# Layer norms cut into 128-token steps, and the last pair of sequences finished in halves

## The chip, the core and the metric

The kernel runs on one core of a Trainium2 chip. A core has five engines with their own instruction queues: PE (matrix products), DVE (vector), ACT (scalar functions), POOL (GpSimd) and SP (here only the issuer of transfers). Each queue runs strictly in order; engines wait for one another through semaphores. Products land in PSUM, which has eight banks of 128 x 512 float32 values; everything else lies in SBUF. The metric is the device time of one execution in microseconds.

## What is computed

Sixteen sequences of 256 tokens with 128 features go through twelve layers of attention without softmax, each with a residual sum, then a layer norm, a gated feed-forward part and a second layer norm:

```python
for i in range(12):
    q, k, v = split(x @ Wqkv[i].T + bqkv[i])          # 16 heads of 8
    att = einsum('bhqd,bhkd->bhqk', q, k) / sqrt(8)
    y = einsum('bhqk,bhkd->bhqd', att, v)
    x = y @ Wproj[i].T + bproj[i] + x
x = layernorm(inputs + x)
h = silu(x @ wg.T) * (x @ wu.T)                        # 384 hidden, weights int / 127
x = layernorm(x + h @ wd.T)
```

Because there is no softmax, the kernel carries, for each sequence, a 128 x 128 matrix that maps the input tokens to the current ones (and one column for the offset), and multiplies the tokens by it only at the end.

## The kernel before

Sequences are taken in eight pairs (p = 0 to 7, 512 tokens each). A prologue computes for each pair the Gram matrix of its tokens (L328), with a column of ones beside the tokens so that the same product gives the token sums. DVE turns them into means (L332 to L334), PE turns the means into rows (L338), and DVE makes the centred Gram matrix g (L345). Twelve layers follow, in two groups of four pairs. Then `ffn` runs once for each pair.

In `ffn`, 512 tokens are four chunks of 128 (K = 4). PE applies the pair's matrix to the tokens (L627 and L629) into one bank; `norm(pr, True)` is the first layer norm. It has three operations: statistics of the four chunks, either all on ACT (L568, squares with an accumulated sum) or all on DVE (four L571 and then four L573); the reciprocal root on POOL (L580 and L581); and the scaling, either on DVE in one instruction over 512 columns (L586) or on ACT in four (L591). PE transposes the result (L635); a copy (L637, ACT or DVE) and a difference on DVE (L638) split it in a high and a low part so that reduced-precision float32 products stay exact. For each of three blocks of 128 hidden units PE makes gate and up (L645, L646), ACT the silu (L648), DVE the product with up (L649), ACT or DVE the high part (L650), POOL or DVE the low part (L651), and PE adds both parts' products to the down bank (L656 to L658). DVE adds the residual (L660), PE transposes back (L664), and `norm(po, False)` is the second layer norm: statistics on DVE alone (L571, L573), the root on POOL, an offset on DVE (L599), and the scaling of the four chunks, all on DVE (L593) or all on ACT (L595). One transfer writes the pair's 512 tokens (L668).

The order of the instructions is not written out. Every operation is handed to `Plan` with a modelled cost for each engine that may run it, the values that it reads and writes, and a priority. `Plan.run` (L113) always takes, among the operations that could end first, the one with the lowest priority number less a small share of the work that hangs on it, gives it to the engine on which it would end first, and emits it there. The priority of a pair's `ffn` is L + FOFF + FSTEP * p (L692), with FSTEP = 0.15. The plan knows of the eight banks only who may hold one: it has no rule on which engines may read one bank at the same time. The semaphores are put in afterwards, by the layer under the kernel, from the tiles that each instruction touches. What stands outside the plan (constants, masks, the memsets of the ones at L265) is placed by that layer.

Of the kernel before, what the change touches and what calls it, by code (L numbers as in the profile page):

```python
# [9 lines left out]
F32 = mybir.dt.float32  # L10
# [3 lines left out]
AF = mybir.ActivationFunctionType  # L14
ALU = mybir.AluOpType
# [6 lines left out]
C = 128  # L22
# [21 lines left out]
LATE = 0.02  # L44
QLATE = 0.3
FOFF = -1
FSTEP = 0.15
LSTEP = 0.05
WLEAD = 0.6
TAILW = 0.0001  # L50
# [38 lines left out]
class Plan:  # L89
    def __init__(self, slots):  # L90
        self.slots, self.ops = slots, []

    def op(self, costs, emit, reads=(), writes=(), prio=0.0):

        o = Op(len(self.ops), costs, emit, prio)
        for v in reads:
            o.deps.update(v.writers)
        for v in writes:
            o.deps.update(v.writers, v.readers)
            v.writers, v.readers = [o], []  # L100
        for v in reads:
            if v not in writes:
                v.readers.append(o)
        o.vals = list(dict.fromkeys([*reads, *writes]))
        for v in o.vals:
            if v.kind:
                v.left += 1
                v.ops.append(o)
        for d in o.deps:
            d.users.append(o)  # L110
        self.ops.append(o)
# [49 lines left out]
def mm32(n=C):  # L161
    return max(220, 4 * n / 2.4 + 8)


def mmr(n):
    return max(111, 0.447 * n + 5)


def act(n, sbuf=False, pointers=0):
    return (94 if sbuf else 51) + 93 * pointers + n / 1.2  # L170


def dve(n, fast=False):
    return 69 + n / (1.92 if fast else 0.96)


def pool(n):
    return 147 + 2.1 * n
# [7 lines left out]
def linear_attention_ffn_kernel(ctx: ExitStack, tc: tile.TileContext, x, xt, wall, wq0, bias, wg, wu, wd, out):  # L186
# [9 lines left out]
    def copy(e, dst, src):  # L196
        if e == ACT:
            nc.scalar.copy(dst, src)  # L198
        else:
            (nc.vector if e == DVE else nc.gpsimd).tensor_copy(dst, src)  # L200

    def sub(e, dst, a, b):
        (nc.vector if e == DVE else nc.gpsimd).tensor_tensor(dst, a, b, ALU.subtract)  # L203
# [5 lines left out]

    zero = new("zero", [128], BF16)  # L210
    nc.vector.memset(zero, 0.0)
    for _ in range(WARM):
        nc.tensor.matmul(banks[7][:, :128], zero, zero, start=True, stop=True)
    tst = new("tst", [B, W])
# [43 lines left out]
        plan.op({SP: kb * 5}, lambda e: nc.sync.dma_start(dst, src), [], vs, prio)  # L258


    qgvs = [new(f"qgv{p}", [PB * W + PB * C]) for p in range(NP)]
    xtoks = [t.rearrange("p (k c) -> p k c", c=C + 1) for t in qgvs]
    vq, vgv = [Val() for _ in range(NP)], [Val() for _ in range(NP)]
    for p in range(NP):
        nc.gpsimd.memset(xtoks[p][:, :, C:], 1.0)  # L265
        load(xtoks[p][:, :, 0:C], x[p * 512 : (p + 1) * 512, :].rearrange("(k p) c -> p k c", p=128), [vq[p], vgv[p]], -9 + 0.01 * p)
        load(xts[p], xt[:, p * PB * T : (p + 1) * PB * T], [vx[p]], 2 + 0.01 * p)

# [279 lines left out]
    def ffn(p, prio):  # L548
# [5 lines left out]
        v = {n: Val() for n in ("cr", "cp", "cq", "tt", "st", "rs", "nb", "x1", "xh", "xl", "sg0", "sg1", "hh0", "hh1", "hl0", "hl1")}  # L554
        v["cp"], v["cq"] = vcp[p % 2], vcq[p % 2]

        def op(costs, emit, reads, writes):
            plan.op(costs, emit, reads, writes, prio)

        def norm(src, centred):  # L560

            xs, rows = t("x1"), lambda: bank(src)
            cut = lambda a, k: a[:, k * C : (k + 1) * C]

            def stats(e):
                if e == ACT:
                    for k in range(K):
                        nc.scalar.activation(cut(xs, k), cut(rows(), k), AF.Square, scale=1 / math.sqrt(C), accum_out=t("mv")[:, k, 1:2])  # L568
                else:
                    for k in range(K):  # L570
                        nc.vector.bn_stats(t("st")[:, k, :], cut(rows(), k))  # L571
                    for k in range(K):
                        nc.vector.bn_aggr(t("mv")[:, k, :], t("st")[:, k, :])  # L573
            costs = {DVE: K * (dve(C) + 70)}
            if centred:
                costs[ACT] = K * (act(C) + 93)
            op(costs, stats, [src], [v["st"], v["x1"]])

            def rstd(e):
                nc.gpsimd.tensor_scalar(t("ve"), t("mv")[:, :, 1], 1.0, EPS, ALU.mult, ALU.add)  # L580
                nc.gpsimd.tensor_tensor(t("rs"), t("ve"), mhalf, ALU.pow)  # L581
            op({POOL: 1220}, rstd, [v["st"]], [v["rs"]])

            def scale(e):
                if centred and e == DVE:
                    nc.vector.tensor_tensor(chunks(xs), chunks(rows()), t("rs").unsqueeze(2).to_broadcast([128, K, C]), ALU.mult)  # L586
                    return
                for k in range(K):
                    d, r, rs = cut(xs, k), cut(rows(), k), t("rs")[:, k : k + 1]
                    if centred:  # L590
                        nc.scalar.activation(d, r, AF.Copy, scale=rs)  # L591
                    elif e == DVE:
                        nc.vector.tensor_scalar(d, r, t("mv")[:, k, 0:1], rs, ALU.subtract, ALU.mult)  # L593
                    else:
                        nc.scalar.activation(d, r, AF.Identity, bias=t("nb")[:, k : k + 1], scale=rs)  # L595
            if centred:
                costs = {DVE: dve(N), ACT: K * act(C, False, 1)}
            else:
                op({DVE: 75}, lambda e: nc.vector.scalar_tensor_tensor(t("nb"), t("mv")[:, :, 0], -1.0, t("rs"), ALU.mult, ALU.mult), [v["rs"], v["st"]], [v["nb"]])  # L599
                costs = {DVE: K * 319, ACT: K * act(C, False, 2)}  # L600
            op(costs, scale, [src, v["rs"], v["st"], v["nb"]], [v["x1"]])


        ptt, pc, pr, px, pd, po = (Val("bank") for _ in range(6))

        def tr_t(e):
            for b in range(PB):
# [20 lines left out]
            for k in range(K):  # L628
                nc.tensor.matmul(bank(pr)[:, k * C : (k + 1) * C], x[:, k * 128 : (k + 1) * 128], t("tt")[:, (k // 2) * C : (k // 2 + 1) * C], start=False, stop=(k == K - 1))  # L629
        op({PE: K * mm32() + mmr(N)}, mm_r, [vx[p], v["tt"], v["cq"]], [pr])  # L630
        norm(pr, True)

        def tr_x(e):
            for k in range(K):
                nc.tensor.transpose(bank(px)[:, k * 128 : (k + 1) * 128], t("x1")[:, k * C : (k + 1) * C], ident)  # L635
        op({PE: K * 109}, tr_x, [v["x1"]], [px])
        op({ACT: act(N), DVE: dve(N)}, lambda e: copy(e, t("xh"), bank(px)), [px], [v["xh"]])  # L637
        op({DVE: dve(N)}, lambda e: nc.vector.tensor_tensor(t("xl"), bank(px), t("xh").bitcast(F32), ALU.subtract), [px, v["xh"]], [v["xl"]])  # L638
        for n in range(NH):
            sg, hh, hlo = f"sg{n % 2}", f"hh{n % NB}", f"hl{n % NB}"  # L640
            pgate, pup = Val("bank"), Val("bank")
            for key, o in (("g", pgate), ("u", pup)):
                def mm_x(e, key=key, o=o, n=n):
                    ws = fw[key][:, n * C : (n + 1) * C]
                    nc.tensor.matmul(bank(o), ws, t("xh"), start=True, stop=False)  # L645
                    nc.tensor.matmul(bank(o), ws, t("xl"), start=False, stop=True)  # L646
                op({PE: 2 * mmr(N)}, mm_x, [v["xh"], v["xl"], vfw[key]], [o])
            op({ACT: act(N)}, lambda e, sg=sg, o=pgate: nc.scalar.activation(t(sg), bank(o), AF.Silu, scale=QSCALE), [pgate], [v[sg]])  # L648
            op({DVE: dve(N)}, lambda e, sg=sg, o=pup: nc.vector.scalar_tensor_tensor(t(sg), bank(o), QSCALE, t(sg), ALU.mult, ALU.mult), [pup], [v[sg]])  # L649
            op({ACT: act(N, True), DVE: dve(N, True)}, lambda e, sg=sg, hh=hh: copy(e, t(hh), t(sg)), [v[sg]], [v[hh]])  # L650
            op({POOL: pool(N), DVE: dve(N)}, lambda e, sg=sg, hh=hh, hlo=hlo: sub(e, t(hlo), t(sg), t(hh).bitcast(F32)), [v[sg], v[hh]], [v[hlo]])  # L651

            def mm_d(e, n=n, hh=hh, hlo=hlo):
                ws = fw["d"][:, n * C : (n + 1) * C]
                if n == 0:
                    nc.tensor.matmul(bank(pd), id127r, t("xl"), start=True, stop=False)  # L656
                nc.tensor.matmul(bank(pd), ws, t(hh), start=False, stop=False)
                nc.tensor.matmul(bank(pd), ws, t(hlo), start=False, stop=(n == NH - 1))  # L658
            op({PE: (2 + (n == 0)) * mmr(N)}, mm_d, [v[hh], v[hlo], v["xl"], vfw["d"]], [pd])
        op({DVE: dve(N)}, lambda e: nc.vector.scalar_tensor_tensor(t("sg0"), bank(pd), QSCALE, t("xh").bitcast(F32), ALU.mult, ALU.add), [pd, v["xh"]], [v["sg0"]])  # L660

        def tr_o(e):
            for k in range(K):
                nc.tensor.transpose(bank(po)[:, k * C : (k + 1) * C], t("sg0")[:, k * 128 : (k + 1) * 128], ident)  # L664
        op({PE: K * 109}, tr_o, [v["sg0"]], [po])
        norm(po, False)
        r0 = p * N
        op({SP: 2.6 * N}, lambda e: nc.sync.dma_start(out[r0 : r0 + N, :].rearrange("(k p) c -> p k c", p=128), chunks(t("x1"))), [v["x1"]], [])  # L668

    prep_weights(0)  # L670
    for p in range(NP):
# [54 lines left out]
```

## Time and profile before

| | |
|---|---|
| median of three runs | 320.36 us (319.89 to 320.46) |
| profiled execution | 319.71 us |
| its span | 317.5 us |
| busy: PE, DVE, ACT, POOL | 304.1, 242.2, 216.2, 142.4 us |
| mean granted PE clock | 0.989 |
| writes of the output | 8 transfers of 256 KB, median 2.3 us from issue to landing |

The span runs from the first to the last recorded event; some 2.2 us of the execution lie outside it. The stages are: the prologue to about 20 us, the layers to about 259 us (the last addition into the sequences' matrices, L516, starts at 259.25 us), the feed-forward parts, which overlap the last layer and go on to about 307 us on PE, and the rest of the norms and the last write. In an answer by line a line of code may stand for a helper: L198, L200, L203 and L206 are copies, differences and products of the kind that the tile names say.

### The profile page before, as it was taken

The page shows a single profiled execution, that of the slowest core. Times are in us where ns is not written, and L with a number is a line of the kernel's source. Part 1 is how long each engine was busy: PE and PEld are TensorE (multiplying, and loading weights), DVE is VectorE, ACT ScalarE, POOL GpSimd, SP SyncE. Part 2 cuts the span into 40 slices and gives each one's busy share as a digit, 9 for nine tenths or more (in the row PEclk, how much of TensorE's full clock was granted, in tenths as well). Part 3 has the DMA queues.
Part 4 walks back from the last instruction along what each step waited for, and adds up shares of the span by engine and source line. Part 5 has one row for each costly group of instructions (what it writes and reads, how often), then busy time and mean ns, then how long its engine had stood idle before and what let it go on. Part 6 is the DMA issues. An engine that isn't in the chain of part 4 may idle for free.

```text
span 317.5 us, 12581 instructions
## 1 busy us (share of the span) xinstructions
PE 304.1 (96%) x5074; PEld 279.8 (88%) x5074; DVE 242.2 (76%) x743; ACT 216.2 (68%) x579; POOL 142.4 (45%) x239
## 2 busy tenths in 40 slices
PE   6999999999999999999999999999999999999970
PEld 6998999999999999999999999999999898888840
DVE  4779688767777677776877768677597698999995
ACT  2458887676776767667676676767687677957651
POOL 6327543326433364233641436313431356658863
PEclk9999999999999999999999999999999999999995
DMA  7463640210201103021030110310000000001124
GB/s 224 111 197 96 173 118 2 51 39 16 72 2 39 51 8 81 2 51 39 2 87 2 39 51 2 76 52 5 3 2 2 2 4 0 2 0 33 35 79 121
DMA packets 22473, 15.64 MB, mean 49 GB/s; under 512 B 1936, under 2 KB 19856, under 8 KB 22416
## 3 DMA queue, kind: packets, MB, share of 16 engines
q1 hardware_dynamic: 22128, 14.75, 17.1%
q8 instruction: 40, 0.66, 0.9%
q14 instruction: 17, 0.14, 0.2%
q10 hardware_dynamic: 288, 0.09, 0.1%
HBM read 8.02 MB, written 2.10 MB: 32 GB/s over the span
## 4 chain that ended last, share of the span: by engine, by line
PE 93%; DVE 4%; POOL 2%; issue 0%; DVEq 0%; POOLq 0%
PE bank L443 14%; PE bank L422 8%; PE bank L492 8%; PE bank L424 7%; PE bank L423 7%; PE bank L482 5%; PE bank L430 5%; PE bank L509 4%; PE bank L510 4%; PE bank L511 4%; PE bank L645 3%; PE bank L432 3%; PE bank L646 3%; PE bank L431 3%; PE bank L328 3%; PE bank L375 3%
## 5 line engine op out<-in xcount | busy, mean ns | idle before, releaser
L203 POOL TENSOR_TENSOR thl<-tst,thl 128x260 fp32r<-128x260 f32 x88 | 68.5, 809 | 32.4 <-ACT thl L198 32.4
L198 ACT COPY qgv<-bank 128x256 f32<-128x256 f32 x174 | 63.0, 373 | 25.6 <-PE bank L432 18.2
L198 ACT COPY kv<-bank 128x512 f32<-128x512 f32 (+1 forms) x92 | 52.4, 573 | 21.1 <-PE bank L424 8.2
L422 PE MATMUL bank<-whl,thl 128*128 128x256 f32 x176 | 51.9, 295 | 0.0
L423 PE MATMUL bank<-whl,thl 128*128 128x256 f32 x176 | 49.5, 281 | 0.0
L424 PE MATMUL bank<-whl,thl 128*128 128x256 f32 x176 | 49.4, 281 | 0.0
L390 POOL TENSOR_SCALAR tst<-tst,bcol 128x8 f32<-128x8 f32 x21 | 7.0, 332 | 94.0 <-PE bank L375 94.0
L443 PE MATMUL bank<-kv,g 128*128 128x128 f32 x352 | 42.9, 275 | 0.0
L198 ACT CAST thl<-tst 128x260 fp32r<-128x260 f32 x88 | 32.3, 409 | 15.3 <-DVE tst L516 15.1
L443 PEld LDWEIGHTS bank<-kv,g 128*128 128x128 f32 x352 | 41.1, 191 | 0.2 <-issue 0.2
L516 DVE TENSOR_TENSOR tst<-bank,tst 128x260 f32<-128x260 f32 x96 | 36.2, 424 | 5.2 <-POOL tst L390 3.2
L200 DVE CAST yhl<-bank 128x260 fp32r<-128x260 f32 x48 | 18.3, 423 | 27.3 <-PE bank L492 27.3
L436 DVE TENSOR_SCALAR qgv<-bank,bcol 128x2 f32<-128x2 f32 x88 | 19.3, 220 | 25.5 <-ACT qgv L198 20.8
L422 PEld LDWEIGHTS bank<-whl,thl 128*128 128x128 f32 x176 | 33.1, 188 | 4.2 <-issue 4.2
L505 DVE TENSOR_TENSOR yhl<-bank,yhl 128x260 fp32r<-128x260 f32 x96 | 34.2, 418 | 0.0
L423 PEld LDWEIGHTS bank<-whl,thl 128*128 128x128 f32 x176 | 33.2, 189 | 0.0
L424 PEld LDWEIGHTS bank<-whl,thl 128*128 128x128 f32 x176 | 33.2, 188 | 0.0
L430 PE MATMUL bank<-thl,whl 128*128 128x260 f32 x88 | 29.0, 330 | 0.0
L492 PE MATMUL bank<-qgv,gm 32*32 32x130 f32 x1536 | 25.9, 280 | 0.0
L198 ACT CAST yhl<-bank 128x260 fp32r<-128x260 f32 (+1 forms) x56 | 20.6, 411 | 7.6 <-PE bank L492 5.9
L432 PE MATMUL bank<-thl,whl 128*128 128x260 f32 x88 | 24.7, 281 | 0.0
L431 PE MATMUL bank<-thl,whl 128*128 128x260 f32 x88 | 24.7, 281 | 0.0
(155 smaller groups left out, 739.0 us busy)
## 6 DMA issues: line engine op xcount, KB each, us to landing
wraw<-wall SPq DMA_DIRECT2D x12, 256.0 KB, 3.4
wpt<-whl SPq DMA_DIRECT2D x24, 96.0 KB, 2.2
qgv<-x SPq DMA_DIRECT2D x8, 256.0 KB, 5.4
xt<-xt SPq DMA_DIRECT2D x8, 256.0 KB, 4.7
out<-kv SPq DMA_DIRECT2D x8, 256.0 KB, 2.3
wpt<-whl SPq DMA_DIRECT2D x24, 64.0 KB, 2.2
wpt<-whl SPq DMA_DIRECT2D x24, 32.0 KB, 1.9
wraw<-wg SPq DMA_DIRECT2D x1, 192.0 KB, 3.8
```

Source lines behind the costliest of these rows:

```text
L198: nc.scalar.copy(dst, src)
L203: (nc.vector if e == DVE else nc.gpsimd).tensor_tensor(dst, a, b, ALU.subtract)
L422: nc.tensor.matmul(o, hi[:, b, 0:C], hl(0, 1, 2), start=True, stop=False)
L423: nc.tensor.matmul(o, hi[:, b, 0:C], hl(1, 1, 2), start=False, stop=False)
L424: nc.tensor.matmul(o, lo[:, b, 0:C], hl(0, 1, 2), start=False, stop=True)
L430: nc.tensor.matmul(o, hl(0, 0), flat(hi), start=True, stop=False)
L431: nc.tensor.matmul(o, hl(0, 0), flat(lo), start=False, stop=False)
L432: nc.tensor.matmul(o, hl(1, 0), flat(hi), start=False, stop=True)
L443: nc.tensor.matmul(bank(pgv)[:, b * C : (b + 1) * C], g0[p][:, b, :], tv(b), start=True, stop=True)
L492: nc.tensor.matmul(bank(pys[r])[group(g + r), b * W : (b + 1) * W], gm[group(g), r * PB + b, :], qss[p][group(g), b, :], start=True, stop= ...
L505: plan.op({DVE: dve(PB * W)}, lambda e: nc.vector.tensor_tensor(yl, bank(py)[:, : PB * W], yh.bitcast(F32), ALU.subtract), [py, vyh[p]], [ ...
L516: plan.op({DVE: dve(PB * W)}, lambda e: nc.vector.tensor_tensor(ts, bank(pw)[:, : PB * W], ts, ALU.add), [pw], [vt[p], vc[p]], prio)
```

## The change

Four things change.

First, `norm` hands the plan each chunk's statistics and each chunk's scaling as an operation of its own. So the chunks of one norm may go to different engines. On DVE a chunk's aggregate (L573) now follows its own statistics (L571) at once, where four of the one were followed by four of the other; the DVE scaling of the first norm is one instruction a chunk in place of one for all four.

Second, the last pair (p = 7) has its third hidden block, its down product, its residual sum, its transposes, its second norm and its output in two halves of 256 tokens. Each half has a down bank and a transpose bank of its own. In this third block the down product is a plain float32 product of the whole value, with no high and low part.

Third, FSTEP goes from 0.15 to 0.3, and the last pair's second and third block and its end get a priority number lower by FLAST = 0.2, which the plan takes sooner.

Fourth, the ones beside the tokens are set by DVE, in the code right after the first memset, and no longer by POOL.

```diff
-FSTEP = 0.15
+FSTEP = 0.3
+FLAST = 0.2
...
     nc.vector.memset(zero, 0.0)
+    qgvs = [new(f"qgv{p}", [PB * W + PB * C]) for p in range(NP)]
+    xtoks = [t.rearrange("p (k c) -> p k c", c=C + 1) for t in qgvs]
+    for t in xtoks:
+        nc.vector.memset(t[:, :, C:], 1.0)
...
-        nc.gpsimd.memset(xtoks[p][:, :, C:], 1.0)
...
-        def norm(src, centred):
+        def norm(src, centred, ks, x1):
...
+            for k, vk in zip(ks, vs):
+                def stats(e, k=k):
+                    if e == ACT:
                         nc.scalar.activation(cut(xs, k), cut(rows(), k), AF.Square, scale=1 / math.sqrt(C), accum_out=t("mv")[:, k, 1:2])
+                    else:
                         nc.vector.bn_stats(t("st")[:, k, :], cut(rows(), k))
                         nc.vector.bn_aggr(t("mv")[:, k, :], t("st")[:, k, :])
-            costs = {DVE: K * (dve(C) + 70)}
+                costs = {DVE: dve(C) + 90}
...
+            for k, vk in zip(ks, vn):
+                def scale(e, k=k):
                     d, r, rs = cut(xs, k), cut(rows(), k), t("rs")[:, k : k + 1]
+                    if e == DVE and centred:
+                        nc.vector.tensor_scalar(d, r, rs, None, ALU.mult)
...
+                costs = {DVE: dve(C) + 60, ACT: act(C, False, 1)} if centred else {DVE: 319, ACT: act(C, False, 2)}
+                op(costs, scale, [src, rs, *vs, nb], [vk])
...
+        halves = [range(K // 2), range(K // 2, K)] if p == NP - 1 else whole
+        pds = [pd] if len(halves) == 1 else [Val("bank") for _ in halves]
         for n in range(NH):
+            parts = halves if n == NH - 1 else whole
+            if p == NP - 1 and n:
+                sooner[0] = FLAST
+            for i, ks in enumerate(parts):
...
+                if plain:
+                    def mm_f(e, n=n, sg=sg, ks=ks, j=i):
+                        nc.tensor.matmul(cols(bank(pds[j]), ks), fw["d"][:, n * C : (n + 1) * C].bitcast(F32), cols(t(sg), ks), start=False, stop=True)
+                    op({PE: mm32(m)}, mm_f, [s, vfw["d"], v[sg]], [pds[i]])
+                    continue
...
+        for i, ks in enumerate(halves):
+            y, po = Val(), Val("bank")
...
+            x2 = norm(po, False, ks, [v["xl"]])
+            r0, r1 = (p * K + ks[0]) * 128, (p * K + ks[-1] + 1) * 128
+            op({SP: 2.6 * m}, lambda e, ks=ks, r0=r0, r1=r1: nc.sync.dma_start(out[r0:r1, :].rearrange("(k p) c -> p k c", p=128), chunks(cols(t("x1"), ks))), x2, [])
```

## The prediction

> **What bounds the kernel.** I read the shares and slices of the page first. PE is busy 96% of the span, so up to about 305 us the kernel seems bound by PE. I then asked for the engines' busy time from the last addition into the sequences' matrices (L516, 259.25 us) on. The columns are start and end, length, then PE, PEld, DVE, ACT and POOL busy.
>
> ```profile
> 259.25:270.00 10.75, 10.75 (x81) 9.24 (x79) 9.90 (x29) 8.68 (x37) 7.62 (x23) 1.00 0.00 2
> 270.00:306.90 36.90, 35.95 (x174) 28.82 (x172) 36.15 (x103) 26.90 (x58) 27.83 (x27) 1.00 0.08 22
> 306.90:314.20 7.30, 1.32 (x9) 0.84 (x8) 7.01 (x34) 1.50 (x4) 3.00 (x5) 0.73 0.45 124
> 314.20:317.50 3.30, 0.00 (x0) 0.00 (x0) 0.00 (x0) 0.00 (x0) 0.00 (x0) 0.50 0.43 123
> ```
>
> From there DVE is busy 9.90 + 36.15 + 7.01 = 53.06 of 54.95 us, and it ends last: PE is done at 306.9, DVE works on to 314.2, and the last write takes the other 3.3. Up to 305 us PE is as full, but its end does not set the kernel's. DVE's queue does: what is added to it after 259 us lengthens the kernel, unless it fits into the 1.9 us of idleness there.
>
> The next rows of the timeline (start, length, engine, line) price DVE work.
>
> ```profile
> 269.78 0.69 DVE L649 SCALAR_TENSOR_TENSOR qgv<-bank,qgv 128x512 f32<-128x512 f32 x1
> 270.51 0.43 DVE L200 CAST hh<-qgv 128x512 fp32r<-128x512 f32 x1
> ...
> 286.39 0.88 DVE L571 BATCH_NORM_STATS2 st<-bank 128x6 f32<-128x128 f32 x4
> 287.19 0.36 DVE L573 BATCH_NORM_AGGREGATE mv<-st 128x2 f32<-128x6 f32 x4
> 287.47 0.66 DVE L203 TENSOR_TENSOR hl<-xt,hh 128x512 fp32r<-128x512 f32 x1
> ```
>
> Four chunks' statistics occupy DVE for 287.47 - 286.39 = 1.08 us, 0.27 a chunk, because independent instructions overlap: L571 starts every 0.20 us though one lasts 0.28. The cast at 270.51 needs the product before it, and starts only 0.04 us after that ends (270.47).
>
> The third view is the list of waits, the fourth the first 9 us.
>
> ```profile
> DVE qgv L436 <- ACT qgv L198: 20.8, 33, 0.9
> ```
>
> ```profile
> 1.59 1.42 DVE L218 COPY tst<-ident 128x2048 f32<-128x2048 f32 x1 [0.61 <-POOL ident masks.py:199]
> 4.89 0.33 POOL L265 MEMSET qgv<- 128x4 f32 x8
> 5.05 3.81 PE L328 MATMUL bank<-qgv 128*128 128x129 f32 x16 [1.70 <-POOL qgv L265]
> 9.32 0.42 DVE L200 COPY kv<-bank 128x256 f32<-128x256 f32 x1 [0.20 <-PE bank L338]
> 11.79 0.15 DVE L332 TENSOR_SCALAR means<-bank 128x2 f32<-128x2 f32 x1
> ```
>
> L436 reads one column of a bank of which ACT's L198 reads the others, and the plan gives it no dependence on that copy. Yet it waited 33 times, 0.63 us in the mean: two engines don't read a bank together here.
>
> **The change, part by part.** I use the order in which the changed kernel is built, and count DVE's instructions behind the last L516 in both.
>
> *Statistics.* 40 chunks in place of 36: four first-norm chunks come over from ACT. Each aggregate now needs the instruction just ahead: 0.28 + 0.04, then 0.07 until the next can start (aggregates start 0.07 apart), 0.39 a chunk. 40 x 0.39 - 9 x 1.08 = +5.9.
> *Scalings.* Four L586 go (each holds DVE 0.60) and four one-chunk ones come at 0.32 (L593: four in 1.36, the last 0.40): -1.1. Second-norm chunks 12 to 14: +0.6.
> *What the plan regroups (FSTEP, FLAST).* Casts cq 4 to 0 at 0.35 (-1.4), hh 9 to 5 at 0.43 (-1.7), one token copy more (+0.35), xh copies 0 to 2 at 0.60 (+1.2), low parts 9 to 11 at 0.62 (+1.2), four small ones more at 0.08 (+0.3).
> *Halves.* Two halves of a 512-column DVE operation hold DVE 2 x 0.35, not 0.60; twice +0.1.
> Sum on DVE: +5.6 us.
>
> What leaves DVE goes to ACT (busy 37.1 of the 54.95 us) and what POOL gains, one more root at 1.0, to POOL (38.5): their idle time covers it; if they are late, DVE waits, see the next term. PE gets two float32 products of 256 columns; L629's float32 rows run 128 columns in 0.22 us, so 2 x 0.45 in place of two at 0.23, +0.4, with nine more issues. PE runs ahead of DVE; without that cover it costs 0.4. The ninth output issue, 0.37 us on SP, lies beside the last half's norm.
>
> *One bank, two engines.* The chunks of a norm share a bank. Behind the last L516, 16 DVE instructions of norms are built with a wait on ACT, seven of them second-norm scalings. No norm of before shows this; the nearest row is L436's. Bounds: none binds, 0, and each at 0.63, +10. For the typical second norm: DVE writes the offset, ACT scales two chunks (0.81 by L595's four in 1.50), two hand-offs at about 0.08; DVE has one 0.65 us low part meanwhile and then stands some 0.3 us in front of its own chunk. Seven times is 2.0, and I let the nine first-norm waits fall where ACT is long done: +2.0.
>
> The Trainium skill, "PSUM — Partial Sum Buffer", section "PSUM bank collisions raise a hardware error", says that any two engines on one bank and 32-partition quadrant, reader with reader too, must be kept apart by semaphores. That speaks against splitting a norm over ACT and DVE: by it all 16 waits are forced, which the L436 row agrees with, but it has no price.
>
> The skill's "VectorE: DVE Perf Modes", section "The DRAIN you can't avoid", says that the pipe empties after every DVE operation anyway and a semaphore costs nothing extra. By that the 0.12 us a chunk for alternating would vanish and the statistics cost +1.1, not +5.9. The 0.20 us starts of 0.28 us instructions contradict it, so I keep +5.9.
>
> *Idle time.* Of DVE's 1.9 us of idleness most is waits for ACT, POOL and PE that a later DVE no longer meets: -1.3, between 0 and -1.9. One matrix-times-tokens stage of PE (1.1 us) moves behind the last L516, DVE has 0.6 us more ahead of it: I take 0, between -1.1 and +1.
>
> *Ones on DVE.* The first transfer is issued at 0.79 and lands 3.2 us later, at 4.0; PE waited for the memsets to 5.05. The eight memsets (0.33 us on POOL) now stand behind DVE's first one, long before 4.0; POOL loses them, SP's order stays. So the Gram products start 1.0 earlier, and the first two pairs' means (7.18, 8.90) too. But in the built order the constants' copies (L218, L240, L244, L250), which stood ahead of all means, now stand behind the second pair's: they start at about 8.05 and hold DVE 1.35 + 0.26 + 0.55 + 0.80 = 3.0, or 2.05 if the two last need only 0.22 without POOL beside them. Behind them wait the copy of 9.32 and what leads to the fourth pair's means (11.79, hence 2.47 later), and PE waits for these. Copy at 10.1 to 11.05 and, since its successors no longer wait 0.2 for PE, the fourth means at 12.4 to 13.3. That is +0.6 to +1.5; if DVE made it up, -1.0. I take +0.6, because PE is full from there to 25 us and can give nothing back, but DVE has slack from 15 us.
>
> *End.* The last chunk goes to ACT behind DVE's chunk of the same bank, +0.5; half a write lands some 0.2 sooner (transfers of 32 to 96 KB: 1.9 to 2.2): +0.3.
>
> Sum: 5.6 + 2.0 - 1.3 + 0.6 + 0.3 = +7.2. The profiled execution took 319.71, span 317.5: 326.9 us. It stands 0.65 below the median of 320.36, within the runs' spread or nearly; a measurement tells about 0.2% (0.64 us) here.
>
> **Rivals.**
> *Alternating is free.* If a chunk costs 0.27 also in turn with its aggregate, 40 x 0.12 = 4.8 go: 322.1. For it: instructions do overlap; against: the 0.04 us behind a dependence.
> *PE sets the end: faster.* Pairs finish further apart, so little DVE work is left at the end: behind the last product with up DVE worked for 11.3 us (302.88 to 314.19) and now has about 5 us of queue. If DVE kept up with PE, the last product would come at 302.9 less 1.0 (start) and the end needs about 12 where it took 14.6: down product 0.7, residuals 0.8, transposes 0.6, four chunks 1.6, root 1.3, scalings 1.3, write 3.3, hand-offs and lag 2.3. That is 3.6 less, 316.1. It decides once DVE's queue behind the last L516 is under 54.9 - 3.6 = 51 us; I count 58.7.
> *Every wait binds* at 0.63: +8 on the forecast, 334.9. Against it: PE and POOL feed ACT late only in a few places of before.
> *The parts cancel*, nothing measurable: 320.4.
>
> **How the numbers follow.** Forecast and its neighbourhood (324 to 331) 0.62; alternating free 0.17; PE sets the end 0.12; cancel 0.04; every wait 0.05. Slower is 0.62 + 0.17 + 0.05 = 0.84, same 0.04, faster 0.12. The range goes from 320.8, which leaves out the two cases below, to 331.0: the statistics' bound below, about four more microseconds of bank waits above.
>
> **What would show it.** Statistics: L571 and L573 in turn, 0.39 us from chunk to chunk. Waits: DVE norm rows released by ACT, together some 2 us or more. Start: first Gram product at about 4.05, the copy into kv near 10.5, the layers' rows some 0.6 late. DVE still over 95% busy from 260 us on, PE with idle stretches it did not have. I am wrong if PE stays full to its end, or if DVE's queue is shorter than counted.

## The result and the profile after

| | before | after |
|---|---|---|
| median | 320.12 us (318.71 to 320.46) | 333.49 us (333.20 to 333.92) |
| profiled execution, span | 319.71, 317.5 us | 333.92, 332.0 us |
| last token addition starts (L516, now L519) | 259.25 us | 260.64 us |
| from there to the end of DVE's last instruction | 54.9 us | 67.5 us |
| from there to the end of the span | 3.3 us | 3.9 us |

The runs of before are those made beside the ones of after. The ratio is 1.0427 (95% interval 1.0393 to 1.0461). The forecast was 326.9 us with a range to 331.0: the side was right, the loss was nearly twice the one forecast, and the time lies outside the range. The three differences in the lower rows, 1.4 + 12.5 + 0.6, make the 14.5 us by which the two spans differ.

First the busy time by stage of the kernel after, cut where the forecast cut it (start and end, length, then PE, PEld, DVE, ACT, POOL busy); in the last stage, to 332.00 us, ACT's last scaling and the writes are left.

```profile
260.64:270.00 9.36, 8.97 (x51) 7.00 (x49) 8.34 (x24) 7.01 (x24) 4.23 (x9) 1.00 0.00 1
270.00:306.90 36.90, 32.76 (x167) 24.41 (x168) 34.51 (x90) 25.86 (x68) 22.10 (x28) 1.00 0.08 22
306.90:328.12 21.22, 12.52 (x58) 9.32 (x58) 18.66 (x63) 9.30 (x20) 7.56 (x12) 0.89 0.13 38
...
```

DVE is busy 8.34 + 34.51 + 18.66 = 61.5 us there, 8.4 more than the 53.1 of before, and stands idle for 6.0 instead of 1.9 (counted from start to start, which takes gaps under 0.15 us as part of the work, 4.4 instead of 1.15). PE, full to 305 us before, now has gaps from the first of these stages on; its longest waits there are for the residual (L687) that DVE hands to its transposes (L691), 4.0 us in three places. So the end is still DVE's, as the forecast had it, but DVE is no longer always busy (91% of 67.5 us, where the forecast had over 95%).

Three groups of rows carry the difference. The first is the timeline of a second norm's statistics (start, length, engine, line).

```profile
286.50 0.27 DVE L577 BATCH_NORM_STATS2 st<-bank 128x6 f32<-128x128 f32 x1
286.80 0.18 DVE L578 BATCH_NORM_AGGREGATE mv<-st 128x2 f32<-128x6 f32 x1
286.90 0.27 DVE L577 BATCH_NORM_STATS2 st<-bank 128x6 f32<-128x128 f32 x1
...
290.46 0.68 DVE L687 SCALAR_TENSOR_TENSOR xt<-bank,yhl 128x512 f32<-128x512 f32 x1
290.76 1.28 POOL L204 TENSOR_TENSOR hl<-xt,hh 128x512 fp32r<-128x512 f32 x1
291.06 0.68 DVE L640 TENSOR_TENSOR thl<-bank,yhl 128x512 fp32r<-128x512 f32 x1
291.66 0.40 DVE L589 SCALAR_TENSOR_TENSOR nb<-mv,rs 128x4 f32<-128x4 f32 x1
291.99 0.68 DVE L204 TENSOR_TENSOR hl<-xt,hh 128x512 fp32r<-128x512 f32 x1
292.94 0.41 DVE L596 TENSOR_SCALAR kv<-bank,mv,rs 128x128 f32<-128x128 f32 x1 [0.27 <-ACT kv L600]
...
304.88 2.96 POOL L204 TENSOR_TENSOR hl<-xt,hh 128x512 fp32r<-128x512 f32 x2
304.91 1.78 DVE L204 TENSOR_TENSOR hl<-qgv,hh 128x512 fp32r<-128x512 f32 x1
306.62 1.23 DVE L589 SCALAR_TENSOR_TENSOR nb<-mv,rs 128x4 f32<-128x4 f32 x1
```

A chunk takes 0.40 us (286.50 to 286.90), as forecast. Then follow two things that the forecast had no row for. The offset nb (L589) works on four columns and takes 0.40 us at 291.66: it ends at 292.06, when POOL's subtraction of 290.76 ends (292.04). At 306.62 it takes 1.23 us and ends at 307.85; POOL's two subtractions end at 307.84. In the row above it DVE's own subtraction takes 1.78 in place of 0.68. The residual (290.46) and the low part xl (291.06) lie beside the same POOL row and keep their 0.68: they read one operand from a bank; nb and hl have all their operands in SBUF. Before, the nb rows took 0.16 us in the mean; now nine take 3.7 us. The lines' own answers, before and after (shortest, median and longest in ns, first and last start):

```profile
L599 DVE SCALAR_TENSOR_TENSOR nb<-mv,rs x8: 120/162/227, 289.3 to 312.7; 128x4 f32<-128x4 f32 x8
...
L589 DVE SCALAR_TENSOR_TENSOR nb<-mv,rs x9: 130/353/1228, 283.1 to 327.7; 128x4 f32<-128x4 f32 x7, 128x2 f32<-128x2 f32 x2
```

The last row of the norm, L596 at 292.94, shows the third thing: it waits 0.27 us for ACT's chunk of the same bank. The list of waits of DVE in the kernel after, first behind the last token addition and then over the whole run, sums these up (us, times, longest).

```profile
DVE kv L596 <- ACT kv L600: 2.5, 7, 0.6
DVE st L577 <- ACT kv L575: 0.7, 3, 0.2
...
DVE st L577 <- ACT kv L575: 2.4, 7, 0.7
DVE kv L594 <- ACT kv L598: 1.5, 3, 0.6
```

Behind the last token addition 3.2 us go to banks that ACT holds. The other 1.7 + 1.5 us of norm waits lie ahead of it, between 248 and 260 us.

### The profile page after: what moved, and what is told of

Read it like the earlier page. It is cut to its first block, busy times and chain, and to the rows that moved or that the text cites. A ratio compares the mean times of both kernels' runs of the same rounds, so it can differ in the third digit from the quotient of the medians.

```text
span 332.0 us, 12627 instructions
## 1 busy us (share of the span) xinstructions
PE 311.2 (94%) x5085; PEld 281.4 (85%) x5085; DVE 249.8 (75%) x770; ACT 221.6 (67%) x580; POOL 138.1 (42%) x233
## 4 chain that ended last, share of the span: by engine, by line
PE 76%; DVE 15%; ACT 3%; issue 2%; POOL 1%; DMA 1%; ACTq 0%; DVEq 0%
PE bank L446 13%; PE bank L425 8%; PE bank L495 7%; PE bank L427 6%; PE bank L426 6%; PE bank L485 5%; PE bank L433 4%; PE bank L512 4%; PE bank L513 3%; PE bank L514 3%; PE bank L435 3%; PE bank L434 3%; PE bank L378 3%; DVE st L577 3%; PE bank L331 2%
## 5 line engine op out<-in xcount | busy, mean ns | idle before, releaser
L199 ACT COPY qgv<-bank 128x256 f32<-128x256 f32 x177 | 64.2, 374 | 23.9 <-PE bank L435 18.1
L201 DVE CAST yhl<-bank 128x260 fp32r<-128x260 f32 (+1 forms) x50 | 19.7, 433 | 26.7 <-PE bank L495 26.7
L519 DVE TENSOR_TENSOR tst<-bank,tst 128x260 f32<-128x260 f32 x96 | 35.9, 422 | 4.7 <-POOL tst L393 3.3
L199 ACT CAST yhl<-bank 128x260 fp32r<-128x260 f32 (+1 forms) x54 | 19.4, 404 | 5.8 <-PE bank L495 5.8
```

The source lines that it names most:

```text
L519: plan.op({DVE: dve(PB * W)}, lambda e: nc.vector.tensor_tensor(ts, bank(pw)[:, : PB * W], ts, ALU.add), [pw], [vt[p], vc[p]], prio)
```

## The experiments

Theory A was that the one-chunk steps of the norms cost the time, on DVE's queue; theory B, that the new order of the pairs and the last pair's halves do. The first four runs take the change apart. "In the kernel before" means that all other parts of the change were put back; the diffs are excerpts, and show a run's kernel against the kernel named unless a note under them says otherwise.

**The changed kernel with grouped norms.** The edit puts the three operations of the old norm back, over the chunks `ks` of a half or a whole pair:

```diff
-            for k, vk in zip(ks, vs):
-                def stats(e, k=k):
+            def stats(e):
...
+                    for k in ks:
+                        nc.vector.bn_stats(t("st")[:, k, :], cut(rows(), k))
+                    for k in ks:
+                        nc.vector.bn_aggr(t("mv")[:, k, :], t("st")[:, k, :])
...
+            op(costs, scale, [src, rs, *vs, nb], vn)
```

> The changed kernel with only its norms put back to one operation over all chunks (four statistics, four aggregates, one scaling on one engine), each half of the last pair in two-chunk groups; ones on DVE, FSTEP, FLAST, halves and the float32 product stay. Theory A (the one-chunk steps cost the time, on DVE's queue behind the last token addition: statistics +6.5 us, waits for a bank +3, collisions with POOL the rest): the loss goes, 320.5 to 321.5 us. Theory B (the new order of the pairs and the last pair's halves cost it): 326 us or more remains.

Measured: 322.71 us, ratio 1.0070 (1.0049 to 1.0092). 10.8 of the 13.4 us are gone; the result lies 1.2 us above the upper bound of theory A, and theory B is out.

**The steps alone**, in the kernel before:

```diff
-FSTEP = 0.3
-FLAST = 0.2
+FSTEP = 0.15
+FLAST = 0.0
...
-        halves = [range(K // 2), range(K // 2, K)] if p == NP - 1 else whole
+        halves = [range(K // 2), range(K // 2, K)] if False else whole
```

(against the changed kernel; the ones are back on POOL too)

> The kernel before with the one-chunk norms alone; ones on POOL, FSTEP 0.15, no halves. Theory A: 326 to 330 us (39 chunks at 0.41 less 9 groups at 1.08 is +6, scalings and casts -2, waits for a bank +2 to +3, collisions 0 to +3). Theory B: 322 to 324 us.

Measured: 328.81 us, ratio 1.0262 (1.0208 to 1.0317). Theory A holds for 8.9 us of the loss; B's number is missed.

**The spacing of the pairs alone**, in the kernel before:

```diff
-FSTEP = 0.15
+FSTEP = 0.3
```

> The kernel before with FSTEP 0.3 alone, so the pairs' ends stand further apart. Behind the last token addition DVE then has one more group of statistics (+1.1 us), five more low parts (+3.1), three casts fewer to hh, four fewer to cq and one scaling fewer (-3.7). Theory A: 320 to 321.5 us. Theory B: 325 us or more.

Measured: 322.23 us, ratio 1.0070 (1.0046 to 1.0094), a miss of 0.7 for theory A. DVE's work behind the last token addition is 53.8 us from start to start, as before, where 0.5 more was counted; its idle time is what grew, by 2.3 (1.15 to 3.48). The waits of DVE behind the last token addition in this run:

```profile
DVE nb L590 <- POOL rs L587: 2.2, 2, 1.4
```

A reading that no run tests: pairs that finish further apart leave DVE with less to do while POOL takes a root, 1.0 us, so it stands in front of nb.

**The last pair's halves alone**, in the kernel before, with all that the change does to the last pair:

```diff
+FLAST = 0.2
...
+        halves = [range(K // 2), range(K // 2, K)] if p == NP - 1 else whole
...
+        pds = [pd] if len(halves) == 1 else [Val("bank") for _ in halves]
...
+                    op({PE: mm32(m)}, mm_f, [s, vfw["d"], v[sg]], [pds[i]])
```

> The kernel before with the last pair's halves, their banks, the float32 product and FLAST alone. Theory A: 319.5 to 321.5 us, the new order of DVE's work nearly cancels (+1.6 low parts and xh, -2.1 scalings and casts). Theory B: 322 us or more. If the shorter end counts, it is under 319.5.

Measured: 319.96 us, ratio 0.9999 (0.9975 to 1.0023): no difference.

**Statistics in turn, nothing else.** In the grouped kernel of the first run one loop is changed:

```diff
                     for k in ks:
                         nc.vector.bn_stats(t("st")[:, k, :], cut(rows(), k))
-                    for k in ks:
                         nc.vector.bn_aggr(t("mv")[:, k, :], t("st")[:, k, :])
```

> The grouped kernel of the first experiment, its work and its plan unchanged, but each chunk's aggregate is issued right behind its statistics instead of behind all four. 32 chunks lie behind the last token addition; in the trace of the changed kernel a chunk in turn holds DVE 0.41 us, four together 0.28 each. Theory A (the alternation itself is paid in full): 322.7 + 32 x 0.13 = 326.9 us, 326 to 328. Rival (DVE had waits of 2.5 us for ACT and POOL behind the aggregates that swallow it, or PE sets the pace): under 324.5.

Measured: 326.00 us, ratio 1.0209 (1.0176 to 1.0243), 3.3 us more than grouped. On DVE the statistics' rows, counted from start to start, took 13.2 us in place of 9.0: the full 32 x 0.13. The time grew by 0.9 us less than these rows did; in the traces DVE idles 0.7 us less than in the grouped kernel (3.2 against 3.9).

**The changed kernel with grouped statistics, scalings still split**, and **with grouped scalings, statistics still split**: one of the two loops is replaced by the old single operation.

```diff
-                op(costs, stats, [src, *x1], [vk])
+            op(costs, stats, [src, *x1], vs)
```

for the first, and for the second

```diff
-                op(costs, scale, [src, rs, *vs, nb], [vk])
+            op(costs, scale, [src, rs, *vs, nb], vn)
```

> The changed kernel with the statistics of a norm in one operation again (four statistics, then four aggregates), the scalings still one chunk at a time on either engine. Eight chunks go back to ACT: 16.6 us of statistics on DVE become 32 x 0.28 = 9.0; two more low parts, two more scalings and one more copy (+2.2), fewer casts (-1.0), no waits of statistics for ACT's squares (-0.7): 326 to 328 us if the statistics are the larger part. If the scalings' waits for a bank are, 330 us or more.

Measured: 324.16 us, ratio 1.0161 (1.0126 to 1.0195): 9.3 us less than the changed kernel, more than expected.

> The changed kernel with each norm's scaling on one engine again, the statistics still one chunk at a time. DVE no longer waits for ACT in front of a scaling (-3.5 us), four 512-column scalings take the place of four one-chunk ones (+1.5), four second-norm chunks go (-1.1): 329.5 to 331.5 us. If bank waits only move to another place, 333 us.

Measured: 327.29 us, ratio 1.0257 (1.0212 to 1.0301): 6.2 us less, where 3 were expected. The two add up to more than the 10.8 us of the first run, so each also removes part of what the other causes. One such part is seen in both traces: the last token addition starts at 258.4 us in either, against 260.64 when both are split. The rows of waits above show DVE standing 3.2 us in norms ahead of it.

**The offset on POOL.** The changed kernel, its plan and order unchanged; POOL makes nb beside the root.

```diff
+                if not centred:
+                    nc.gpsimd.tensor_scalar(t("nm")[:, kk], t("mv")[:, kk, 0], -1.0, 0.0, ALU.mult, ALU.add)
                 nc.gpsimd.tensor_tensor(t("rs")[:, kk], t("ve")[:, kk], mhalf[:, kk], ALU.pow)
+                if not centred:
+                    nc.gpsimd.tensor_tensor(t("nb")[:, kk], t("nm")[:, kk], t("rs")[:, kk], ALU.mult)
...
+                op({DVE: 75}, lambda e: None, [rs, *vs], [nb])
```

> The changed kernel, its plan and order unchanged, but the second norm's offset nb is made by POOL (two small operations beside the root) and not by DVE. Theory A (DVE instructions whose operands all lie in SBUF stand still while POOL subtracts two tensors: the nine nb rows took 3.7 us, the longest 1.23 ending with POOL's low part): the wait passes on to the next such instruction in four places, is gone in the longest, and ACT's chunks start earlier: 331 to 332.3 us. Rival (those rows waited for the root, or the time is hidden): 333 us or more.

Measured: 331.71 us, ratio 1.0407 (1.0358 to 1.0456). Counted from start to start, the eight rows hl<-xt,hh went from 5.7 to 8.2 us while the 2.9 us of nb were gone: the wait passed on to the next instruction with all its operands in SBUF, as theory A said. The 1.8 us gained are the longest nb row, behind which no such instruction stood, and 0.6 us less of waiting for ACT, whose chunks get their offset sooner.

**Bare costs**, in blocks behind the last write of the kernel before (one execution; `sync` is a short hand-over that lets both engines start together):

```diff
+        on_dve("sbuf", 4)
+        sync()
+        on_pool(3)
+        for kind, n in (("sbuf", 4), ("bank", 6), ("cast", 6), ("small", 6)):
+            sync()
+            on_pool(3)
+            on_dve(kind, n)
...
+            for k in range(K):
+                if k % 2:
+                    nc.vector.tensor_scalar(cut(dst[1], k), cut(src[1], k), mrs[:, k : k + 1], None, ALU.mult)
+                else:
+                    nc.scalar.activation(cut(dst[0], k), cut(src[0], k), AF.Copy, scale=mrs[:, k : k + 1])
```

> The kernel before with blocks of single operations behind its last write (its own time is longer by them and not of interest). DVE and POOL work on 128x512 tensors in SBUF, alone and together; ACT and DVE scale four chunks in turn. Theory A: alone a DVE subtraction holds DVE 0.60 us and POOL's 1.25; together, DVE instructions with all operands in SBUF stand still while POOL's runs, so four DVE and three POOL subtractions take about 4 x 0.60 + 3 x 1.25 = 6.2 us; with one operand in a bank DVE keeps 0.60 and the block 3.8; six small ones of 128x4 take 0.5 us without a wait, but last to the end of a POOL instruction. Rival (no exclusion): 3.8 us in all blocks. Statistics: four chunks 1.1 us in groups, 1.6 in turn. Scalings in turn: from one bank each needs the one before, 4 x 0.4 = 1.6 us and more; from two banks about 0.9, also where both engines write the same tile.

The timeline of these blocks, without the small copies that separate them:

```profile
317.08 2.49 DVE L719 TENSOR_TENSOR xt<-xt,xt 128x512 f32<-128x512 f32 x4
...
320.26 3.70 POOL L728 TENSOR_TENSOR qgv<-xt,xt 128x512 f32<-128x512 f32 x3
...
324.63 4.62 DVE L719 TENSOR_TENSOR xt<-xt,xt 128x512 f32<-128x512 f32 x4
...
325.31 5.05 POOL L728 TENSOR_TENSOR qgv<-xt,xt 128x512 f32<-128x512 f32 x3
...
331.04 3.67 DVE L721 TENSOR_TENSOR xt<-bank,xt 128x512 f32<-128x512 f32 x6
...
331.32 3.72 POOL L728 TENSOR_TENSOR qgv<-xt,xt 128x512 f32<-128x512 f32 x3
...
341.41 1.59 DVE L725 SCALAR_TENSOR_TENSOR small<-xt,xt 128x4 f32<-128x4 f32 x6
...
341.71 3.70 POOL L728 TENSOR_TENSOR qgv<-xt,xt 128x512 f32<-128x512 f32 x3
...
346.08 0.88 DVE L740 BATCH_NORM_STATS2 mst<-bank 128x6 f32<-128x128 f32 x4
...
349.50 0.36 ACT L755 ACTIVATE qgv<-bank,mrs 128x128 f32<-128x128 f32 x1
...
349.90 0.35 DVE L753 TENSOR_SCALAR qgv<-bank,mrs 128x128 f32<-128x128 f32 x1
350.28 0.37 ACT L755 ACTIVATE qgv<-bank,mrs 128x128 f32<-128x128 f32 x1 [0.42 <-DVE qgv L753]
350.69 0.35 DVE L753 TENSOR_SCALAR qgv<-bank,mrs 128x128 f32<-128x128 f32 x1 [0.44 <-ACT qgv L755]
...
351.28 0.62 ACT L755 ACTIVATE qgv<-bank,mrs 128x128 f32<-128x128 f32 x2
...
351.48 0.60 DVE L753 TENSOR_SCALAR qgv<-bank,mrs 128x128 f32<-128x128 f32 x2
```

Four DVE subtractions alone take 2.49 us, three of POOL's 3.70. Together, all in SBUF, they take from 324.63 to 330.36, 5.7 us: close to the sum of 6.2. While both run, they take turns, one instruction each: DVE's and POOL's both start 1.7 us apart, where a pair one after the other would take 0.60 + 1.22. With one operand in a bank six of DVE's take 3.67 beside POOL's 3.72; neither notices the other. Of six instructions on four columns five start 0.07 us apart; the sixth, beside POOL's first subtraction, takes 1.23 us and ends at 343.00, when that ends (342.98). Six copies within SBUF take 5.29 beside POOL's 4.26, which takes 3.70 alone, so these slow each other too; the first two, ahead of POOL's start, are 0.33 us apart, the next three 1.4. Statistics of four chunks held DVE 1.08 us in groups (346.08 to 347.16, the next instruction) and 1.62 in turn (347.63 to 349.25). Scalings in turn from one bank start 0.40 us apart (349.50, 349.90, 350.28, 350.69) and take 1.54 in all; from two banks they run side by side in 0.80. Both pairs of blocks were also run with two destination tiles in place of one, at the same times: the bank sets the wait, not the tile written. These are waits that the kernel is built with; what the two engines would do on one bank without them no run shows.

Two pages of the Trainium skill bear on these blocks. In "VectorE: DVE Perf Modes", section "The DRAIN you can't avoid", the sentence that a semaphore between two DVE operations costs nothing extra would make groups and turns cost the same; 1.08 against 1.62 us says otherwise here. The same section also says that a next operation that is not held starts earlier, and the grouped statistics, 0.20 us apart at 0.28 each, agree with that. "SBUF — State Buffer", section "SBUF: two separate sides", describes a port pair that DVE and GpSimd hold exclusively for a whole instruction, when DVE runs a two-port mode, or reads two SBUF inputs while GpSimd reads SBUF; the blocks agree with it, 5.7 us together, where 2.5 and 3.7 alone.

**Ones on DVE alone**, in the kernel before:

```diff
+    for t in xtoks:
+        nc.vector.memset(t[:, :, C:], 1.0)
...
-        nc.gpsimd.memset(xtoks[p][:, :, C:], 1.0)
```

> The kernel before with the ones set by DVE alone. The prediction's term: +0.6 us (320.7). The trace of the changed kernel, where the layers ran 0.15 us earlier: -0.1 to -0.2 us, no difference that can be measured.

Measured: 319.60 us, ratio 1.0011 (0.9988 to 1.0034): no difference.

**Two attempts at less work for DVE**, in the kernel before. The first takes DVE from the choice for the casts to hh, the second from the choice for the low parts hl:

```diff
-                op({ACT: act(m, True), DVE: dve(m, True)}, lambda e, sg=sg, hh=hh, ks=ks: copy(e, cols(t(hh), ks), cols(t(sg), ks)), [s, *then(hh)], [h, *full(hh)])
+                op({ACT: act(m, True)}, lambda e, sg=sg, hh=hh, ks=ks: copy(e, cols(t(hh), ks), cols(t(sg), ks)), [s, *then(hh)], [h, *full(hh)])
...
-                op({POOL: pool(m), DVE: dve(m)}, lambda e, sg=sg, hh=hh, hlo=hlo, ks=ks: sub(e, cols(t(hlo), ks), cols(t(sg), ks), cols(t(hh), ks).bitcast(F32)), [s, h, v[sg], *then(hlo)], [lo, *full(hlo)])
+                op({POOL: pool(m)}, lambda e, sg=sg, hh=hh, hlo=hlo, ks=ks: sub(e, cols(t(hlo), ks), cols(t(sg), ks), cols(t(hh), ks).bitcast(F32)), [s, h, v[sg], *then(hlo)], [lo, *full(hlo)])
```

> The kernel before with the casts to hh on ACT alone. Behind the last token addition DVE loses nine casts (-4.2 us) and, as the plan puts it, gains two low parts (+1.2), four second-norm chunks (+1.2) and one scaling (+0.6). If DVE's queue sets the end: -1.2 us, 318.8. If DVE then waits for ACT's casts: 320 or more.

Measured: 319.02 us, ratio 0.9977 (0.9964 to 0.9990): 0.9 us faster than before, the only gain found.

> The kernel before with the low parts hl on POOL alone. DVE loses nine subtractions (-5.6 us) and gains two copies to xh and one cast (+1.7). If DVE's queue sets the end and POOL keeps up: 316 to 317 us. If POOL's exclusion of DVE costs what moves away (nine more subtractions of 1.25 us, each in the way of what DVE does in SBUF), or PE waits for the low parts: 320 us or more.

Measured: 323.01 us, ratio 1.0100 (1.0080 to 1.0119), slower although DVE has nine subtractions less. The groups of rows on DVE behind the last token addition show why (busy, mean ns of one, idle time before):

```profile
L590 DVE SCALAR_TENSOR_TENSOR nb<-mv,rs 128x4 f32<-128x4 f32 x8 | 5.3, 664 | 1.9 <-POOL rs L587 1.8
L201 DVE CAST hh<-xt 128x512 fp32r<-128x512 f32 x7 | 5.1, 722 | 0.2
```

So does the answer for the line itself (shortest, median and longest in ns, first and last start):

```profile
L590 DVE SCALAR_TENSOR_TENSOR nb<-mv,rs x8: 121/588/1247, 292.9 to 316.7; 128x4 f32<-128x4 f32 x8
```

An instruction on four columns takes up to 1.25 us, which is the length of one of POOL's subtractions, and the casts to hh<-xt take 722 ns where 503 before. That PE waits for the low parts is not the reason: its waits in this stretch, 5.4 us, are for DVE, and only a weight load waited for a low part of POOL's, once, 0.3 us.

**What the steps and the spacing lose together.** The steps alone lose 8.9 us and the spacing 2.3, together with two parts that lose nothing 13.4. The changed kernel with the spacing taken back:

```diff
-FSTEP = 0.3
+FSTEP = 0.15
```

> The changed kernel with FSTEP 0.15 again; steps, halves and ones stay. The steps alone gave 328.8 us; the spacing alone +2.3; together with halves and ones 333.5. Theory C (the spacing puts POOL's subtractions in the way of DVE's SBUF instructions, and that is what the steps and the spacing lose only together): 328 to 330 us, and the rows nb and hl at their bare 0.07 and 0.60 us. Rival (steps and halves disturb each other, the spacing is only one more +2.3): 331 us, with the collisions still there.

Measured: 331.36 us, ratio 1.0375 (1.0357 to 1.0393). The rows nb and hl went nearly as theory C said, the time as its rival. From start to start the rows nb and hl exceed their bare 0.07 and 0.60 us by 1.0 us in all, against 4.3 in the changed kernel. But the last token addition moved to 262.02 us, 1.4 later, and the waits for a bank of ACT's grew from 3.2 to 4.5. So neither holds alone.

**Casts on ACT and halves together**, the halves' edit and the first line of the casts' in the kernel before:

```diff
+        halves = [range(K // 2), range(K // 2, K)] if p == NP - 1 else whole
...
-                op({ACT: act(m, True), DVE: dve(m, True)}, lambda e, sg=sg, hh=hh, ks=ks: copy(e, cols(t(hh), ks), cols(t(sg), ks)), [s, *then(hh)], [h, *full(hh)])
+                op({ACT: act(m, True)}, lambda e, sg=sg, hh=hh, ks=ks: copy(e, cols(t(hh), ks), cols(t(sg), ks)), [s, *then(hh)], [h, *full(hh)])
```

> The kernel before with the casts to hh on ACT alone and the last pair's halves. The casts on ACT alone gave 319.0 us, the halves alone no difference. If the two add: 318.5 to 319.5 us; if the halves' new order takes the gain back: 320 or more.

Measured: 320.00 us, ratio 1.0013 (0.9997 to 1.0029). The gain of the casts does not stay beside the halves.

The table puts the traces side by side: start of the last token addition, time from there to DVE's end, DVE's waits for ACT in front of norm rows there (by the timeline), and what the rows nb and hl took above 0.07 and 0.60 us each, from start to start less idle time.

| kernel | last addition | to DVE's end | waits for ACT | nb and hl in excess |
|---|---|---|---|---|
| before | 259.25 | 54.9 | 0 | 0.4 |
| after | 260.64 | 67.5 | 3.2 | 4.3 |
| grouped norms | 259.38 | 59.1 | 0 | 2.2 |
| steps alone | 260.37 | 63.2 | 3.9 | 0.1 |
| spacing alone | 258.88 | 57.3 | 0 | 1.6 |
| halves alone | 259.65 | 55.9 | 0 | 0.4 |
| grouped statistics | 258.40 | 60.5 | 2.1 | 3.1 |
| grouped scalings | 258.39 | 63.1 | 0.7 | 2.6 |
| after, FSTEP 0.15 | 262.02 | 63.8 | 4.5 | 1.0 |

## Why the prediction was too low

*What bounds the kernel* was right: DVE's queue behind the last token addition sets the end, and what is put into it lengthens the kernel. But the queue's length was taken as the sum of its instructions at the durations that they have in the trace of before, and that is where the sum fell short.

*Statistics, +5.9.* Right. From start to start they went from 10.05 to 16.58 us, +6.5, 0.41 a chunk where 0.39 was forecast. The bare blocks show that the turn itself costs 0.54 for four chunks.

*Scalings, -1.1 and +0.6.* A little better than forecast: -0.8 together.

*What the plan regroups.* The counts were right; the durations of two kinds of row were not. "Low parts 9 to 11 at 0.62" and "four small ones more at 0.08", one of them an nb, missed 1.7 us in the low parts and 2.2 in nb: eleven low parts took 8.6 us, 0.78 each, and nine nb 2.9, 0.33 each. This is the step that failed on DVE's side: behind 0.62 stood the rows of before, where only 0.4 us of collisions occur in nb and hl, and I took an instruction's duration as its own, not as a matter of what POOL does at that moment. At the start I had not: the constants' copies are priced there at 0.22 "without POOL beside them", and behind the last token addition the same effect was put at nothing without a reason. The sentence that ACT's and POOL's idle time "covers" what they gain was wrong for POOL in the same way: POOL is less busy after than before (33.9 against 38.5 us behind the last token addition), and yet it costs DVE more.

DVE's term thus was +9.3 instead of +5.6 (63.07 us of work from start to start, 53.79 before).

*One bank, two engines, +2.0.* The mechanism was right, the size not: 3.2 us behind the last token addition. Seven second-norm scalings waited 2.5 us, as many as forecast, at 0.36 in place of 0.3; the first-norm waits, taken at nothing, cost 0.7 there.

*Idle time, -1.3.* Wrong sign. DVE's idle time grew by 3.3 us (from start to start, 1.15 to 4.41), as much as the bank waits; nothing was absorbed in sum. The waits of before for POOL, ACT and PE gave way to others as long, 1.3 us for POOL and PE.

*Where the last token addition lands, 0.* It came 1.4 later, above the upper bound of +1. The bound looked at PE's stage and at DVE's instructions, not at waits. The traces put first-norm chunks in front of it that wait 3.2 us for ACT, and it is late only in the kernels where statistics and scalings are both split (260.3 to 262.0, otherwise 258.4 to 259.7). That the waits are the cause was not tried by itself.

*Ones, +0.6.* Wrong. The first Gram product started at 4.03 us, as forecast, but the constants' copies cost less than the lower of the two counts. In the timeline of the start after:

```profile
8.03 1.22 DVE L224 COPY tst<-ident 128x2048 f32<-128x2048 f32 x1
9.16 0.25 DVE L246 CAST identb<-ident 128x128 bf16<-128x128 f32 x1
9.30 0.22 DVE L250 CAST centerr<-center 128x128 fp32r<-128x128 f32 x1
9.44 0.22 DVE L256 CAST id127r<-id 128x128 fp32r<-128x128 f32 x1
9.57 0.41 DVE L201 COPY kv<-bank 128x256 f32<-128x256 f32 x1
```

Counted from start to start the four hold DVE 1.54 us, where I had added up durations to 2.05 or 3.0. The copy into kv comes at 9.57 (10.1 to 11.05 forecast), the layers start 0.15 us late instead of 0.6 and end as much early, and alone the edit changes nothing that can be measured.

*End, +0.3.* Measured +0.6.

By the traces, then: 9.28 + 3.26 + 1.39 + 0.57 = 14.50 us between the spans, where the forecast had 5.6 + (2.0 - 1.3) + (0 + 0.6) + 0.3 = 7.2. Of the 7.3 missed, about 3.9 are DVE's collisions with POOL, 1.2 the bank waits, 1.4 the idle time counted as absorbed, 0.8 the later token addition; the rest nearly cancels. This is the account of one pair of traces, not what each part is worth by itself: with the spacing taken back the collisions fell by 3.3 us and the time by 2.1.

*The rivals.* "Alternating is free" fell with the run that alternates and does nothing else, +3.3 us. "PE sets the end" fell: DVE's length came to 67.5 us, not below 51. "Every wait binds", 334.9, is nearest in number by luck, and not what happened: ten of the 16 bound, with 0.32 us in the mean, not 0.63. A rival was missing: that DVE's instructions get longer through what POOL runs beside them.

## What to carry to other kernels

A duration read off a profile is that of one neighbourhood: before moving work, note for each row which engine runs what beside it, and which operands lie in SBUF and which in a bank. Work given to the less busy engine is not free where that engine shuts out the one that sets the end, so count the work of both in one sum when both use SBUF operands alone. Keep the parts that one engine reads from a bank together: cutting a step finer gave the planner more freedom and took 0.13 us a chunk for the turn and some 0.3 us for each change of hands.

## What the runs showed of the hardware that was not expected

DVE and POOL hold each other up, for all but some 0.14 us of an instruction (pairs 1.68 us apart where 0.60 + 1.22 would be 1.82), when the operands of both all lie in SBUF: 5.7 us together where 2.5 and 3.7 us alone, and no effect (3.67 beside 3.72 us) when one of DVE's operands is in a bank. An instruction of 0.07 us can so last 1.23. A profile shows such a wait as busy time of the instruction, with no idle time and no releaser, so the list of waits misses it; it is seen by comparing minimum and maximum of a line, 121 and 1247 ns for one and the same form. ACT and DVE, built to take turns on one bank, start 0.40 us apart, 1.54 us for four chunks, and 0.80 from two banks, whichever tile they write.
